# First stage: latents turned by one VectorE transpose and 32 DMAs per block in place of four TensorE transposes

## The chip, the cores and the metric

The kernel runs on one core of a Trainium2 chip. The metric is the device time of one execution in microseconds, the median of several runs; lower is better. The engines are named as in the profile: PE (TensorE matmul) with PEld (its weight loads), DVE (VectorE), ACT (ScalarE), POOL (GpSimd) and SP (SyncE, here only a queue that issues DMAs).

## The reference

The model is two layers over x of 16 x 256 x 256 in float32: a cross-attention of a resampler, a mixture of experts with two of eight experts per token, a second cross-attention, and a gated linear attention. Only the first cross-attention matters here. For each of the 16 batch entries it computes

```python
l = layer_norm(layernorm(x), ln2_g, ln2_b)          # latents, 256 x 256
c = layer_norm(ctx_1024, ln1_g, ln1_b)              # context, 77 x 256
q = l @ Wq                                          # 16 heads of 64
k, v = split(concatenate([c, l], axis=1) @ Wkv)     # 333 keys and values
out = softmax(q k^T / 8) v @ Wo
x = x + tanh(g_xattn[0]) * out
```

Every product contracts over the 256 features, so the normed latents are needed with the features on the partitions: 256 tokens x 256 features have to be turned. After the turning each feature is one partition, and the gain and bias of the second norm are one multiplication and one addition per partition.

## The kernel before

All of it is float32. The first stage (`stage0_fast`) goes through 64 units (b, g): batch entry b from 0 to 15 and, inside it, group g of four heads from 0 to 3. A unit has scores and their exponentials (`scores`), sums of the exponentials on POOL (`sums`), the values of the unit before it (`values`: PE products `o`, then a reciprocal `rd` and a product `oT` on DVE), and the queries and keys of the next unit (`heads`: PE products `qk`, copied by ACT and DVE). The other work is hung between these by hand. Unit (b, 1) also turns the latents of b + 1 (`turn`) and projects the output of b - 1 (`project`); unit (b, 2) computes the values' operands of b + 1 (`all_values`: PE products `v` from the turned latents `kvT`). The routing of the second layer for b - 1, b - 2 and b - 3 is spread over the units by three tables, which `run` reads: `ahead_of` (ahead of the scores), `behind_scores` and `behind_values`, lines 763 to 769. In unit (b, 2), for instance, `ahead_of` puts `route.weigh` and `route.stats`, short DVE work, which ends with the `mv` of the statistics, ahead of the scores.

What is recorded on an engine through `dve`, `act`, `pool` and `pe` keeps the program's order on that engine (`Pinned`, line 42; nearly all of it shows up under line 50). SP's DMAs (`nc.sync`) are not tied; a scheduler places them, and each waits for the DMA eight before it.

`turn(b)`, line 612, is what the change touches. `normed_all` (line 604) has left the latents of b in `xn`, two tiles of 128 tokens x 256 features, on ACT. PE turns them by four 128 x 128 transposes into a PSUM pair named `tr`, and DVE scales the two halves from there into `kvT[b][:, k, :256]` with gain and bias (line 627). The context's rows come 128 at a time, so only ten of the 16 entries bring new ones (0, 1, 3, 4, 6, 8, 9, 11, 13, 14). For these, PE transposes `cn` too, twice, into the same pair, DVE scales them into `ctxT`, and the values of the context (`v` from `ctxT`) come ahead of the values of the latents. ACT copies an entry's context columns from `ctxT` to the end of its `kvT` (line 633). `y`, line 601, is the result of the first of the two norms; its buffer has one slot, written by `normed_y(b + 2)` in unit (b, 3) and last read by `normed_all(b + 1)` in unit (b, 0).

In the last stage the same kind of turning stands already (`turn_ahead`, line 1685): one DVE transpose of all 32 x 32 squares of 128 x 512, then 16 DMAs of 32 partitions x 4 x 32 elements that carry the squares to their places.

Of the kernel before, what the change touches and what calls it, by code (L numbers as in the profile page):

```python
# [10 lines left out]
F32 = mybir.dt.float32  # L11
I32 = mybir.dt.int32
AF = mybir.ActivationFunctionType
ALU = mybir.AluOpType
# [3 lines left out]
P = 128  # L18
B, S, D = 16, 256, 256
# [4 lines left out]
V_LN1G, V_LN1B, V_LN2G, V_LN2B, V_QB, V_KB, V_NW, V_ONE, V_GATE, V_N = 0, 2, 4, 6, 8, 10, 12, 13, 14, 18  # L24
# [49 lines left out]
def layers(ctx: ExitStack, tc: tile.TileContext, t, out, check):  # L74
    nc = tc.nc
# [6 lines left out]
    def const(name, shape, dtype=F32):  # L82
        return cp.tile(list(shape), dtype, tag=name, name=name)
# [30 lines left out]
    def c_count(j):  # L114
        return min(P, c_rows - P * j)

    def c_pieces(b):

        lo, hi = b * S2, (b + 1) * S2
        return [(j, max(lo, P * j) - P * j, max(lo, P * j) - lo, min(hi, P * j + P) - max(lo, P * j))  # L120
                for j in range(lo // P, (hi - 1) // P + 1)]
# [7 lines left out]
    vec = const("vec", [P, V_N])  # L129
# [34 lines left out]
    ident = const("ident", [P, P])  # L164
# [10 lines left out]
    dve, act, pool, pe = (Pinned(tc, x) for x in (nc.vector, nc.scalar, nc.gpsimd, nc.tensor))  # L175
# [43 lines left out]
    def normed(dst, src, mv, rs, p=P, n=2):  # L219
        for i in range(n):  # L220
            act.activation(dst[:, i, :], src[:, i, :], AF.Identity, bias=rs[:p, 1, i:i + 1],
                           scale=rs[:p, 0, i:i + 1])
# [36 lines left out]
    NK, KC = S + S2, 111  # L259
# [289 lines left out]
    if fast:  # L549
        route = Route()  # L550
# [15 lines left out]
    def stage0_fast():  # L566
        with ExitStack() as sx:
            w1 = sx.enter_context(tc.tile_pool(name="f0w1", bufs=1, reuse_waits="tile"))
            w2 = sx.enter_context(tc.tile_pool(name="f0w2", bufs=2, reuse_waits="tile"))
# [3 lines left out]
            def pair(name):  # L573
                return pairs.tile([P, 2, 512], F32, tag="ps", name=name)
# [6 lines left out]
            xn, cn, kvT, v, oT, ctxT = {}, {}, {}, {}, {}, {}  # L581
# [5 lines left out]
            y, mvs, tallies = {}, {}, []  # L587
# [16 lines left out]
            def normed_all(b):  # L604
                xn[b] = w1.tile([P, 2, D], F32, tag="xn", name="xn")
                normed(xn[b], y.pop(b), *mvs.pop((b, "y")))
                if b in c_new:
                    n = c_count(c_new[b])
                    cn[b] = w1.tile([P, 1, D], F32, tag="cn", name="cn")
                    normed(cn[b][:n], cs[b][:n].unsqueeze(1), *mvs.pop((b, "c")), n, 1)  # L610

            def turn(b):
                kvT[b] = w2.tile([P, 2, NK], F32, tag="kvT", name="kvT")
                both = pair("tr")
                j = c_new.get(b)
                n = 0 if j is None else c_count(j)
                for k in range(2):
                    ps = both[:, k, :]
                    for i in range(2):
                        pe.transpose(ps[:, i * P:(i + 1) * P], xn[b][:, i, k * P:(k + 1) * P], ident)  # L620
                    if n:
                        pe.transpose(ps[:, S:S + n], cn[b][:n, 0, k * P:(k + 1) * P], ident[:n, :n])
                if n:
                    ctxT[j] = w2.tile([P, 2, P], F32, tag="ctxT", name="ctxT")
                for k in range(2):
                    ps = both[:, k, :]
                    dve.tensor_scalar(kvT[b][:, k, :S], ps[:, :S], vec[:, V_LN2G + k:V_LN2G + k + 1],
                                            vec[:, V_LN2B + k:V_LN2B + k + 1], ALU.mult, ALU.add)
                    if n:
                        dve.tensor_scalar(ctxT[j][:, k, :n], ps[:, S:S + n], vec[:, V_LN1G + k:V_LN1G + k + 1],  # L630
                                                vec[:, V_LN1B + k:V_LN1B + k + 1], ALU.mult, ALU.add)
                for j, at, to, n in c_pieces(b):
                    act.copy(kvT[b][:, :, S + to:S + to + n], ctxT[j][:, :, at:at + n])
# [120 lines left out]
            def project(b):  # L754
                both = pair("proj")
                for i in range(2):
                    for m in range(8):
# [3 lines left out]


            ahead_of = {0: [(norm_y, 1), (route.exps, -2)], 1: [(route.choose, -2)],
                        2: [(route.weigh, -2), (route.stats, -1)], 3: [(route.place, -2), (norm_x, 2), (norm_c, 2)]}
            behind_scores = {0: [(normed_all, 1), (route.scatter, -3, 1)],
                             1: [(route.scatter, -3, 2)],
                             2: [(route.norm, -1), (route.scatter, -3, 3)],
                             3: [(normed_y, 2), (route.scatter, -2, 0)]}
            behind_values = {2: [(route.ranks, -2, bank)], 3: [(route.logits, -1, bank)]}

            def run(steps, b, g):
                for f, d, *a in steps.get(g, ()):
# [14 lines left out]
            warm(y[0][:, 1, :], 3)  # L787
            normed_all(0)
            turn(0)
            all_values(0)  # L790
            heads(0, 0, 0)
# [3 lines left out]
            for n, (b, g) in enumerate(units):  # L795
# [20 lines left out]
                if g == 1 and b + 1 < B:  # L816
                    turn(b + 1)
# [34 lines left out]
    if fast:  # L852
        stage0_fast()
        s_banks = ctx.enter_context(ExitStack())
        pss = s_banks.enter_context(tc.tile_pool(name="f012ps", bufs=4, space=PSUM, reuse_waits="tile"))

        def shared_bank(name):
            return pss.tile([P, 512], F32, tag="ps", name=name)

    else:  # L860
        stage0()
# [1389 lines left out]
```

## Time and profile before

| | |
|---|---|
| three runs | median 1838.59 us, 1833.2 to 1842.05 |
| the profiled execution | 1836.71 us, its span 1834.8 us |
| granted PE clock in it | 0.995 |
| first stage, from the weights in place | 85 to 960 us |
| turning in the first stage | 64 transposes of latents and 20 of context rows on PE, 32 scalings of 128 x 256 on DVE |

The page lists the busy time of each engine, the course of it over the span, and the groups of instructions by kind. Start times count from the beginning of the span. A group's line gives its number of instructions, its busy time, the mean duration of one, and the idle time of the engine ahead of it with the one that ended it. A busy PE is not a PE at its peak: matmuls overlap, so the price of one is the distance from its start to the next.

### The profile page before, as it was taken

To read this page: it belongs to the slowest core of one execution; us is meant where nothing else is said; L and a number is where in the kernel's file an instruction comes from. 1 tells how busy PE (TensorE), PEld (TensorE's weight loads), DVE (VectorE), ACT (ScalarE), POOL (GpSimd) and SP (SyncE) were. 2 spreads that over 40 slices of the span, in tenths; PEclk is the share of its full clock that TensorE was granted. 3 is DMA by queue.
4 is the path that set the end of the run, shared out by engine and by line. 5 is a ranking of instruction groups with operands and counts; after the bars stand their busy time and mean duration, and the time that the engine had idled before them with its cause. 6 is when DMAs were issued, how large, how long until landed. Compare 5 with 4: busy or idle time off the path is not lost.

```text
span 1834.8 us, 35411 instructions
## 1 busy us (share of the span) xinstructions
PE 1802.7 (98%) x13930; PEld 1246.4 (68%) x13930; DVE 1138.6 (62%) x2695; ACT 832.4 (45%) x1727; POOL 1014.3 (55%) x1001
## 2 busy tenths in 40 slices
PE   8999999999999999999999999999999999999997
PEld 5666666666666666666777866656777777777775
DVE  3345656666656666666475388866666666666664
ACT  4433345343453334434343488744543454445432
POOL 3654766567666576656743766314454445444533
PEclk9999999999999999999999999999999999999999
DMA  9800010000010000000067933100111111111110
GB/s 298 235 1 22 16 35 13 28 17 20 27 35 10 29 20 10 28 24 17 13 221 246 251 56 48 21 3 11 38 28 36 29 37 28 34 31 32 33 31 26
DMA packets 110361, 98.05 MB, mean 53 GB/s; under 512 B 43835, under 2 KB 97763, under 8 KB 109673
## 3 DMA queue, kind: packets, MB, share of 16 engines
q1 hardware_dynamic: 97897, 78.91, 14.5%
q0 software_dynamic: 12288, 16.79, 4.5%
q8 instruction: 112, 1.84, 0.4%
q14 instruction: 64, 0.52, 0.1%
HBM read 52.03 MB, written 38.41 MB: 49 GB/s over the span
## 4 chain that ended last, share of the span: by engine, by line
PE 84%; POOL 7%; DVE 3%; issue 2%; ACT 2%; SPq 1%; DMA 1%; POOLq 0%; ACTq 0%; DVEq 0%
PE o L50 11%; PE qk L50 11%; PE v L50 9%; PE sc L50 8%; PE proj L50 7%; PE kq L1637 6%; PE sc L1637 6%; PE gq L1637 4%; POOL es L50 4%; PE ex L50 3%; PE v L1637 3%; PE o L1637 3%; PE proj L1637 2%; PE low L1637 2%; PE gz L1637 2%
## 5 line engine op out<-in xcount | busy, mean ns | idle before, releaser
L50 POOL TENSOR_SCALAR rs<-mv 128x2 f32<-128x2 f32 (+2 forms) x85 | 16.2, 190 | 404.4 <-DVE mv L50 402.6
L50 DVE RECIPROCAL rd<-o 128x256 f32<-128x256 f32 x64 | 112.3, 1754 | 155.0 <-PE o L50 155.0
L50 ACT ACTIVATE e<-sc 128x1024 f32<-128x1024 f32 (+1 forms) x192 | 181.5, 1015 | 18.5 <-PE sc L50 18.5
L50 POOL TENSOR_TENSOR at<-at,at 128x768 f32<-128x768 f32 x63 | 114.1, 1812 | 134.3 <-DVE at L50 134.3
L50 PE MATMUL sc<-qk 64*128 64x256 f32 (+1 forms) x1536 | 183.1, 384 | 0.5 <-DVE qk L50 0.5
L50 PE MATMUL o<-e,v 128*32 128x256 f32 (+1 forms) x3072 | 177.9, 379 | 0.0
L50 PEld LDWEIGHTS sc<-qk 64*128 64x128 f32 (+1 forms) x1536 | 132.0, 172 | 55.1 <-issue 26.8
L50 POOL TENSOR_TENSOR esum<-esum,es 128x512 f32<-128x512 f32 x128 | 163.2, 1275 | 10.0
L50 PE MATMUL qk<-kvT,wkv 128*128 128x333 f32 x512 | 164.3, 443 | 0.0
L50 POOL TENSOR_TENSOR es<-e 128x1024 f32<-128x1024 f32 x64 | 151.3, 2364 | 12.0 <-ACT e L50 9.0
L50 ACT ACTIVATE qk<-qk 128x256 f32<-128x256 f32 x128 | 48.7, 381 | 232.2 <-PE qk L50 232.2
L50 POOL TENSOR_TENSOR es<-es,e 77x1024 f32<-77x1024 f32 x64 | 150.3, 2349 | 5.0
L50 PEld LDWEIGHTS o<-e,v 128*32 128x32 f32 (+1 forms) x3072 | 99.8, 110 | 66.4
L50 DVE TENSOR_TENSOR at<-sc,amask 128x768 f32<-128x768 f32 x64 | 61.2, 957 | 133.7 <-PE sc L1637 78.2
L50 PE MATMUL qk<-kvT,wq 128*128 128x256 f32 x512 | 134.6, 385 | 0.0
L50 DVE COPY qk<-qk 128x333 f32<-128x333 f32 x128 | 64.6, 505 | 94.8 <-ACT qk L50 93.4
L50 POOL DMA_INDIRECT x<-rows_out,pos x64 | 100.9, 1577 | 35.6 <-issue 16.5
L50 PEld LDWEIGHTS qk<-kvT,wq 128*128 128x128 f32 x512 | 94.3, 189 | 35.1 <-issue 9.6
L50 PEld LDWEIGHTS qk<-kvT,wkv 128*128 128x128 f32 x512 | 97.2, 190 | 30.0
L50 PE MATMUL proj<-wo0h,oT 128*128 128x256 f32 x512 | 113.7, 380 | 0.3 <-DVE oT L50 0.3
L50 PE MATMUL v<-wkv,kvT 128*128 128x512 f32 x256 | 113.1, 595 | 0.0
L50 PEld LDWEIGHTS proj<-wo0h,oT 128*128 128x128 f32 x512 | 96.0, 190 | 13.9 <-issue 0.8
(267 smaller groups left out, 3920.8 us busy)
## 6 DMA issues: line engine op xcount, KB each, us to landing
rows<-zero SPq DMA_DIRECT2D x16, 640.0 KB
xin<-rows SPq DMA_DIRECT2D x16, 640.0 KB
r<-rms SPq DMA_DIRECT2D x30, 256.0 KB
rows_out<-y SPq DMA_DIRECT2D x16, 384.0 KB
v<-vctx SPq DMA_DIRECT2D x15, 308.0 KB
x<-in_x_dram SPq DMA_DIRECT2D x16, 256.0 KB
rows_out<-y SPq DMA_DIRECT2D x16, 256.0 KB
out_dram<-x SPq DMA_DIRECT2D x15, 256.0 KB
```

The lines of the kernel that those rows point to most:

```text
L50: x = getattr(self.engine, name)(*a, **k)
L1637: tc.keep_in_program_order(nc.tensor.matmul(*a, **k))
```

## The change

For entries b of 2 and more the latents are no longer turned on PE. `squares_moved(b + 1)` runs behind the values in unit (b, 0): one DVE transpose turns each of the 64 squares of 32 x 32 of the 128 x 512 tile, each at its own position, into `z` (named `turned`, in the buffer of `y`), and 32 DMAs on SP's queue carry the squares to their places in `kvT`, each DMA taking the two squares that lie at the same place in the two halves of the features, 32 partitions x 2 x 32 elements. `scaled(b + 1)` runs in unit (b, 2), behind `route.weigh` and `route.stats` and ahead of that unit's scores in the program's order: two DVE operations multiply and add in place in `kvT`. `turn` keeps the transposes of context rows, and for b below 2 all of it as it was.

```diff
+            def squares_moved(b):
+
+                if b < 2:
+                    return
+                z = w1.tile([P, 2 * D], F32, tag="y", name="turned")
+                dve.transpose(z, xn[b].rearrange("p i d -> p (i d)"))
+                kvT[b] = w2.tile([P, 2, NK], F32, tag="kvT", name="kvT")
+                to, at = kvT[b][:, :, :S].rearrange("p k (i s) -> p i k s", i=2), z.rearrange("p (i k d) -> p i k d", i=2, k=2)
+                for q in range(0, P, 32):
+                    for r in range(0, P, 32):
+                        for i in range(2):
+                            nc.sync.dma_start(out=to[r:r + 32, i, :, q:q + 32], in_=at[q:q + 32, i, :, r:r + 32])
+
+            def scaled(b):
+
+                if b < 2:
+                    return
+                for k in range(2):
+                    dve.tensor_scalar(kvT[b][:, k, :S], kvT[b][:, k, :S], vec[:, V_LN2G + k:V_LN2G + k + 1],
+                                      vec[:, V_LN2B + k:V_LN2B + k + 1], ALU.mult, ALU.add)
+
             def turn(b):
-                kvT[b] = w2.tile([P, 2, NK], F32, tag="kvT", name="kvT")
-                both = pair("tr")
                 j = c_new.get(b)
                 n = 0 if j is None else c_count(j)
+                if b < 2:
+                    kvT[b] = w2.tile([P, 2, NK], F32, tag="kvT", name="kvT")
+                if b < 2 or n:
+                    both = pair("tr")
                 for k in range(2):
-                    ps = both[:, k, :]
-                    for i in range(2):
-                        pe.transpose(ps[:, i * P:(i + 1) * P], xn[b][:, i, k * P:(k + 1) * P], ident)
+                    for i in range(2 if b < 2 else 0):
+                        pe.transpose(both[:, k, i * P:(i + 1) * P], xn[b][:, i, k * P:(k + 1) * P], ident)
                     if n:
-                        pe.transpose(ps[:, S:S + n], cn[b][:n, 0, k * P:(k + 1) * P], ident[:n, :n])
+                        pe.transpose(both[:, k, S:S + n], cn[b][:n, 0, k * P:(k + 1) * P], ident[:n, :n])
...
-                for k in range(2):
+                for k in range(2 if b < 2 or n else 0):
                     ps = both[:, k, :]
-                    dve.tensor_scalar(kvT[b][:, k, :S], ps[:, :S], vec[:, V_LN2G + k:V_LN2G + k + 1],
-                                            vec[:, V_LN2B + k:V_LN2B + k + 1], ALU.mult, ALU.add)
+                    if b < 2:
+                        dve.tensor_scalar(kvT[b][:, k, :S], ps[:, :S], vec[:, V_LN2G + k:V_LN2G + k + 1],
+                                          vec[:, V_LN2B + k:V_LN2B + k + 1], ALU.mult, ALU.add)
...
-                        2: [(route.weigh, -2), (route.stats, -1)], 3: [(route.place, -2), (norm_x, 2), (norm_c, 2)]}
+                        2: [(route.weigh, -2), (route.stats, -1), (scaled, 1)], 3: [(route.place, -2), (norm_x, 2), (norm_c, 2)]}
...
-            behind_values = {2: [(route.ranks, -2, bank)], 3: [(route.logits, -1, bank)]}
+            behind_values = {0: [(squares_moved, 1)], 2: [(route.ranks, -2, bank)], 3: [(route.logits, -1, bank)]}
```

## The prediction

> **What bounds the kernel now.** I read the page's busy shares first, then the busy time by stretch, TensorE's waits in the first stage, the chain that ended last, and at the end one block of the first stage on the time axis.
>
> ```profile
> PE 1802.7 (98%) x13930; PEld 1246.4 (68%) x13930; DVE 1138.6 (62%) x2695; ACT 832.4 (45%) x1727; POOL 1014.3 (55%) x1001
> ...
> PE 84%; POOL 7%; DVE 3%; issue 2%; ACT 2%; SPq 1%; DMA 1%; POOLq 0%; ACTq 0%; DVEq 0%
> ```
> ```profile
> 85.00:960.00 875.00, 871.64 (x7121) 586.82 (x7120) 536.89 (x1324) 356.11 (x693) 560.31 (x501) 1.00 0.10 30
> ```
> ```profile
> PE o L50 <- POOL es L50: 1.8, 8, 0.4
> PE rank L50 <- DVE hs L50: 0.4, 1, 0.4
> ```
>
> The second fence's columns are the stretch in us, its length, the busy time of PE, PEld, DVE, ACT and POOL, the clock and the DMA share. From 85 to 960 us, the first stage once the weights are in, PE is busy 871.6 of 875 us at full clock. Its longest wait in total there is 1.8 us for POOL's sums (last fence: total, times, longest). The DMA engines stand at 10%. So this stage is paced by PE's own work. An instruction taken from PE is worth its PE time, as long as nothing new makes PE wait.
>
> **What goes.** Block 7 (latents of b = 7, turned in unit (6,1)) brings no new context rows. This is its part of PE's timeline, with the group of these transposes by tile above it:
>
> ```profile
> L50 PE MATMUL tr<-ident,xn x128: 271/273/332, 9.2 to 1190.0; 128*128 128x128 f32 x128
> ```
> ```profile
> 376.13 2.78 PE L50 MATMUL o<-e,v 128*32 128x256 f32 x48
> 378.85 0.66 PE L50 MATMUL tr<-ident,xn 128*128 128x128 f32 x4
> 379.34 7.07 PE L50 MATMUL proj<-wo0h,oT 128*128 128x256 f32 x32
> ```
>
> The 273 ns of one transpose overlap the next; its price is the step from start to start. Four cost 379.34 - 378.85 = 0.49 us. In blocks with context rows six span 0.71 us, 0.11 us a step, and two remain, so 0.44 us goes. Of the 14 blocks (2 to 15), 8 are of the second kind: 8 x 0.44 + 6 x 0.49 = 6.5 us. VectorE loses two PSUM-to-SBUF scalings of 0.53 us per block; they lie beside the 7 us projection, so that is worth nothing. Nor is the freed PSUM pair: PE shows no wait for a bank.
>
> **What is added and moved, in block 7.** The path is new: VectorE transpose, 32 DMAs on SP's queue, VectorE scaling, then PE's value matmuls. These are the places it has to fit into:
>
> ```profile
> 370.65 0.69 DVE L50 TENSOR_TENSOR oT<-o,rd 128x512 f32<-128x512 f32 x1
> 371.43 0.51 DVE L50 COPY qk<-qk 128x333 f32<-128x333 f32 x1
> ...
> 393.53 0.30 DVE L50 BATCH_NORM_AGGREGATE mv<-bst 128x2 f32<-128x6 f32 x2
> 396.41 1.76 DVE L50 RECIPROCAL rd<-o 128x256 f32<-128x256 f32 x1 [2.58 <-PE o L50]
> ```
> ```profile
> 395.66 1.08 POOL L50 DMA_INDIRECT rows<-xw,pos  x1 [0.18 <-issue]
> 396.77 2.36 POOL L50 TENSOR_TENSOR es<-e 128x1024 f32<-128x1024 f32 x1
> ```
>
> The transpose stands behind oT (ends 371.34); the scaling stands behind the last mv (ends 393.83) and ahead of rd. VectorE is idle there for 2.58 us.
>
> The last stage already turns its input this way, with 16 DMAs per block, so durations are to be had:
>
> ```profile
> L50 DVE STREAM_TRANSPOSE turned<-xn x14: 699/711/712, 1258.4 to 1740.6; 128x512 f32<-128x512 f32 x14
> ```
> ```profile
> 1335.18 10.32 SPq L1693 DMA_DIRECT2D xnT<-turned  x16
> ```
> ```profile
> 1346.97 0.89 PE L1637 MATMUL low<-xnT,la 128*128 128x256 f32 x3 [0.23 <-DMA xnT<-turned]
> ```
>
> *Transpose:* 0.71 us, to 372.05. It holds back the first key copy, 371.43 to about 372.05; that then ends at 372.56, ahead of the scores at 372.89 that read it. Cost 0, cover 0.3 us. Its input from ScalarE is ready 0.3 to 3.5 us ahead of it in every block.
>
> *DMAs:* 16 issues take 10.32 us, 0.645 each. The last of the 16 starts at about 1344.9 and PE goes on at 1346.97, so landing takes 2.1 us. The new DMAs move half the pieces each (32 x 2 x 32 against 32 x 4 x 32). The nearest rows are flat in size, as SP's `low` copy of 64 pieces took 0.60 us, so I take 0.645; low end 0.58 (SP's `lowd` copy, 0.54, and 0.04 between two). A few issues of the last stage were 0.1 to 0.7 us late, which I book as 0.3 us per block. First issue at 372.1, last start 31 x 0.645 = 20.0 later at 392.1, landed at 394.2 to 394.5. Nothing urgent stands behind them on SP's queue: in block 6 the next entries, context writes, come at 343.0, and SP would be done at 334. The context load ahead of them goes out within 0.2 us of oT's end (312.54 against 312.43 in block 6).
>
> *Scaling:* PE's 0.49 us lets VectorE reach it at 393.3, so it waits about 1 us for the DMAs. Queued behind it are rd and oT, wanted at 396.41 - 0.49 = 395.9, and PE's value matmuls, wanted at the same time. Two scalings SBUF to SBUF: between the one such row of this width (gbo, 0.35 us) and what they took from PSUM (0.53); I take 0.4 as in the same form with two scalars (xn, 0.41). They end at 395.0 to 395.3, 0.6 to 0.9 us early. In blocks with context rows the values of the context come first (3.5 us), and the cover is wider.
>
> *Waits:* in program order the first value matmul now carries waits for four DMA semaphores more. A wait on PE's queue takes 0.05 us in this trace, so 0.2 us per block if all is exposed and none if PE's queue runs ahead. I take 0.1 in the six blocks that have no context values before it: 0.6 us.
>
> Sum: 6.5 - 0.6 = 5.9 us less, with ends of 3.6 and 6.5. The profiled execution took 1836.7 us (span 1834.8), which gives 1830.8; it lies 1.9 us under the median of the three runs, so the median goes from 1838.6 to 1832.7.
>
> **Where a rule speaks against it.** The Trainium skill, "DMA: Bandwidth & Descriptors", section "Rules for kernel authors", has small transfers coalesced, since under 64 KB one pays mostly overhead; these are 8 KB. If each paid the 2.1 us that the trace shows to landing one after the other, 32 would take 67 us, 43 us past the 24 us from 372 to 396, and 14 blocks would lose some 600 us. The row (16 in 10.32 us) shows the overhead overlapped, with only the issue in series. I take the row.
>
> For a late scaling there is no row. VectorE's transposes took 0.71 us beside POOL and the same without, while its operations with two SBUF inputs were held until POOL's ended:
>
> ```profile
> L50 DVE TENSOR_TENSOR h<-rq,rc x32: 174/1120/3107, 142.5 to 954.7; 128x16 f32<-128x16 f32 x32
> ```
>
> "SBUF — State Buffer", section "Who interferes with whom", says that a `tensor_scalar` between SBUF tensors may take the port pair shared with POOL, and that whichever of the two comes second is blocked for the whole instruction. By the transposes' row a late scaling costs its lateness alone; by the rule and h's row up to 3.1 us more. No trace here shows it for this form; I take the rule for the rival below.
>
> **Rivals.**
> 1. *Likeliest, 0.55:* all of it hides, 1832.7.
> 2. *Part of the gain comes back, 0.22:* the DMAs land 0.5 to 1.5 us later in some blocks. Six blocks without context values at about 1 us each take 6 us back: 1838.6. For it: a cover of only 0.6 to 0.9 us. Against it: the even pace of 0.645.
> 3. *Late landing meets POOL, 0.15, slower:* POOL's scatter starts at 395.66 - 0.49 = 395.2 and its es add ends at 399.13 - 0.49 = 398.6. If the DMAs land after 395.2, an issue pace of over 0.67 us, the first scaling is held to 398.6 and the second ends at 399.4 or later. PE stands from 395.9, 3.5 us in each of six blocks = 21 us; the eight others want the latents 3.5 us later and just escape. Less the 5.9: 1854. Held a second time, to the end of the next add (2.35 us), it is 1868.
> 4. *The change doesn't do what it says, 0.08:* PE's saved time reappears as a wait for POOL, whose sums already hold PE up to 0.4 us in the unit ahead of the transposes: 1838.6. Against it: after them POOL has 9 us of slack, and its next chain starts from VectorE work that PE paces.
>
> **How the numbers follow.** About 0.5% (9 us) is what a measurement of this kernel can tell from no change. The likeliest case lies 5.9 us under the median, inside that bound, and the three runs spread over 9 us. So 0.17 of the 0.55 may read as faster, and nothing else does; rival 3 and a tail of rival 2 make slower 0.16; the rest, 0.67, is within it. The range runs from 1826 (largest gain and a low draw) to 1847; above it lies most of rival 3.
>
> **What would show it.** PE's list should have 56 fewer transposes and no wait of values for kvT over 0.3 us. SP should show 32 issues in about 20.6 us per block. The scaling should take 0.35 to 0.45 us, after an idle time of about 1 us put down to the DMAs, and rd should keep its wait for PE. Wrong would be an issue pace over 0.67, scalings of over 1 us, or rd starting without a wait for PE.

## The result and the profile after

The changed kernel took 1851.91 us, median of 5 runs (1848.18 to 1852.93), beside 1838.34 us for the kernel before (5 runs, 1833.2 to 1842.05): ratio 1.0073, 95% interval 1.0055 to 1.0091. By the medians that is 13.6 us slower, where 1832.7 was predicted. The profiled execution took 1851.91 us, its span 1850.0 us.

The page's busy times and the chain of the changed kernel:

```profile
PE 1803.1 (97%) x13874; PEld 1239.9 (67%) x13874; DVE 1166.5 (63%) x2709; ACT 834.0 (45%) x1727; POOL 1015.5 (55%) x1001
...
PE 74%; SPq 8%; POOL 6%; DVE 5%; issue 2%; DMA 2%; ACT 1%; DVEq 0%; POOLq 0%; ACTq 0%
```

PE's list has the 56 transposes fewer, 13874 against 13930, but its busy time is the same: some products take longer, where the clock falls (below). SP's queue has come into the chain: 8% against 1%, so the chain now runs through the issuing of DMAs. The same two views of the first stage as before, stretch and PE's waits (total, times, longest):

```profile
85.00:970.00 885.00, 869.77 (x7030) 578.70 (x7029) 559.58 (x1311) 354.07 (x685) 559.40 (x499) 0.99 0.12 32
```
```profile
PE v L50 <- issue: 6.7, 3, 2.9
PE v L50 <- DVE kvT L50: 4.8, 5, 1.8
PE o L50 <- POOL es L50: 2.0, 8, 0.4
```

PE stands 15 us of this stretch where it stood 3. Two lines are new, 11.5 us in eight waits, all ahead of the values `v`, which read the scaled latents. A wait put down to "issue" has no releaser in the trace; these stand at the same place as the others, ahead of the same products.

By stages: the first product `ex` of the second layer starts at 934.30 us before and at 949.99 after, 15.7 later. From there to the last stage's first product `low` it is 266.4 and 266.5 us, from there to the end 634.1 and 633.5. So all of the lost time lies in the first stage, and there in five of 14 blocks. (The equal times of the last stage hide a difference. Leaving out the last 7 us of both, the kernel before ran there for 10.2 us at half clock and the changed one not at all; its waits of `low` for turned input are longer, 6.1 us in total against 3.7. The second question below comes back to this.) The period of a block (first projection to first projection), and in the changed kernel the time of the first scaling and both durations, in us from the start of the block's transpose:

| block | before | after | difference | first scaling at | both took |
|---|---|---|---|---|---|
| 2 | 55.10 | 58.82 | +3.7 | 24.17 | 1.19, 2.50 |
| 5 | 55.48 | 55.17 | -0.3 | 23.43 | 0.41, 0.41 |
| 6 | 58.44 | 59.05 | +0.6 | 24.89 | 3.22, 2.49 |
| 7 | 55.48 | 62.00 | +6.5 | 25.04 | 2.61, 2.49 |
| 10 | 55.47 | 55.16 | -0.3 | 23.63 | 0.41, 0.41 |
| 12 | 55.48 | 57.28 | +1.8 | 23.96 | 0.41, 3.36 |
| 15 | 54.51 | 60.95 | +6.4 | 25.16 | 2.48, 2.49 |

Blocks 3, 4, 8, 9, 11, 13 and 14, all with context rows, gained 0.42 to 0.50 each. In blocks without context rows PE wants the scaled latents 24.7 after the transpose, in the others 28.7. Block 3's scalings were slow too (2.49, 2.50), at no cost, since PE wants them so much later there. Gains of 3.9 and losses of 19.1 make 15.2 of the 15.7.

Block 7 is the clearest. VectorE, POOL and PE there, on the time axis:

```profile
396.38 0.30 DVE L50 BATCH_NORM_AGGREGATE mv<-bst 128x2 f32<-128x6 f32 x2
...
398.52 1.08 POOL L50 DMA_INDIRECT rows<-xw,pos  x1 [0.17 <-issue]
...
399.53 5.02 DVE L50 TENSOR_SCALAR kvT<-kvT,vec 128x256 f32<-128x256 f32 x2 [2.86 <-DMA kvT<-turned]
399.63 2.35 POOL L50 TENSOR_TENSOR es<-e 128x1024 f32<-128x1024 f32 x1
402.06 2.34 POOL L50 TENSOR_TENSOR es<-es,e 77x1024 f32<-77x1024 f32 x1
```
```profile
399.00 0.29 PE L50 MATMUL rank<-before,hs 128*32 128x64 f32 x8
402.24 1.85 PE L50 MATMUL v<-wkv,kvT 128*128 128x512 f32 x2 [2.94 <-issue]
404.61 2.07 PE L50 MATMUL v<-wkv,kvT 128*128 128x512 f32 x2 [0.51 <-DVE kvT L50]
```

The last `mv` ends at 396.68. VectorE then waits 2.86 us for the DMAs, and the two scalings, 0.41 us each where nothing disturbs them, take 5.02 together, 2.61 and 2.49 in the table. The first starts just ahead of POOL's first `es` addition and ends 0.16 us behind it, at 402.14; the second ends 0.15 us behind the second addition, at 404.55. PE, done at 399.29, waits 2.94 us and 0.51 more for the second half. An undisturbed block, 10, for comparison:

```profile
576.59 0.73 DVE L50 TENSOR_SCALAR kvT<-kvT,vec 128x256 f32<-128x256 f32 x2 [1.46 <-DMA kvT<-turned]
577.70 1.76 DVE L50 RECIPROCAL rd<-o 128x256 f32<-128x256 f32 x1 [0.38 <-PE o L50]
```

2.94 and 0.51 do not make 6.5. The rest is in PE's clock, last but two of the columns (PEclk), in block 7 before, during and after the wait:

```profile
388.00:399.20 11.20, 11.20 (x110) 7.83 (x108) 4.71 (x20) 4.83 (x9) 3.00 (x6) 1.00 0.09 13
402.20:409.10 6.90, 6.35 (x8) 2.23 (x9) 6.78 (x11) 0.00 (x0) 4.73 (x3) 0.52 0.00 0
409.10:420.00 10.90, 10.90 (x54) 6.80 (x56) 6.88 (x25) 6.30 (x14) 0.00 (x0) 0.99 0.00 0
```

After the wait PE runs at half clock for 6.8 us, which is 3.4 us of work lost. 2.94 + 0.51 + 3.4 less the 0.3 that undisturbed blocks of this kind gain is the 6.5 of the table. Block 15 repeats it; block 2 has 3.4 us at half clock.

### The profile page after: what moved, and what is told of

It reads as the page before. It is cut to its first block, busy times and chain, and to the rows that moved or that the text cites. A ratio compares the mean times of both kernels' runs of the same rounds, so it can differ in the third digit from the quotient of the medians.

```text
span 1850.0 us, 35901 instructions
## 1 busy us (share of the span) xinstructions
PE 1803.1 (97%) x13874; PEld 1239.9 (67%) x13874; DVE 1166.5 (63%) x2709; ACT 834.0 (45%) x1727; POOL 1015.5 (55%) x1001
## 3 DMA queue, kind: packets, MB, share of 16 engines
q8 instruction: 111, 1.82, 0.4%
## 4 chain that ended last, share of the span: by engine, by line
PE 74%; SPq 8%; POOL 6%; DVE 5%; issue 2%; DMA 2%; ACT 1%; DVEq 0%; POOLq 0%; ACTq 0%
PE o L50 10%; PE qk L50 9%; PE v L50 9%; PE sc L50 7%; PE proj L50 5%; PE kq L1660 5%; SPq L623 5%; PE sc L1660 5%; PE gq L1660 3%; PE ex L50 3%; POOL es L50 3%; SPq L1716 3%; PE v L1660 3%; PE o L1660 2%; PE proj L1660 2%
## 5 line engine op out<-in xcount | busy, mean ns | idle before, releaser
L50 ACT ACTIVATE e<-sc 128x1024 f32<-128x1024 f32 (+1 forms) x192 | 181.6, 1016 | 18.1 <-PE sc L50 18.1
L50 PE MATMUL v<-wkv,kvT 128*128 128x512 f32 x256 | 121.9, 628 | 11.5 <-issue 6.7
```

The source lines that it names most:

```text
L50: x = getattr(self.engine, name)(*a, **k)
```

## The experiments

Three theories stood after this profile. **1:** the DMAs land late, and POOL's additions then hold the scaling ("two-port" in the texts below: the plain form, which by the rule weighed in the prediction may take the port pair shared with POOL). **2:** late landing alone stops PE. **3:** what is added costs everywhere, by its mere presence. Where not said otherwise a kernel is an edit of the changed one. "Stage end" is the start of the first `ex`: 934.30 before, 949.99 after.

**Without the turning (no_turn).**

```diff
-                z = w1.tile([P, 2 * D], F32, tag="y", name="turned")
-                dve.transpose(z, xn[b].rearrange("p i d -> p (i d)"))
...
-                            nc.sync.dma_start(out=to[r:r + 32, i, :, q:q + 32], in_=at[q:q + 32, i, :, r:r + 32])
+                if b >= 2:
+                    kvT[b] = kvT[b - 2]
...
```

The entry `(scaled, 1)` goes from the table as well.

> This leaves the turning of the latents out for entries of 2 and more (they take those of two entries before), and with it the transpose, the DMAs and the scaling; the context is turned as before. All theories: what PE's transposes were worth, 6 us under the kernel before, about 1832. If it is 1836 or more, the transposes were never worth their time and the change could not have gained.

Measured: 5569.45 us. The total says nothing: with stale latents it goes through further layers after the first pass (832 products `ex` against 320). Its first pass can be read: stage end 929.39, 4.9 us ahead of before. That is all that PE's transposes were worth in this stage, against 6.5 in my sum (5.9 after the waits that I allowed for).

**Without gain and bias (no_scale).**

```diff
-                        2: [(route.weigh, -2), (route.stats, -1), (scaled, 1)], 3: [(route.place, -2), (norm_x, 2), (norm_c, 2)]}
+                        2: [(route.weigh, -2), (route.stats, -1)], 3: [(route.place, -2), (norm_x, 2), (norm_c, 2)]}
```

> This leaves the gain and bias of the second norm out for entries of 2 and more; transpose and 32 DMAs stay, and the values wait for the DMAs directly. Theory 1 (the scaling comes late and is then held by POOL's additions): no scaling, no hold, so 1832 to 1836. Theory 2 (the DMAs' landing is late enough by itself to stop PE): 1846 to 1852, as with the scaling. Theory 3 (the added transposes and DMAs slow other work everywhere): 1846 to 1852, spread over all blocks.

Measured: 1836.32 us (20 runs) beside 1836.31, ratio 0.9999 [0.9990, 1.0007]; stage end 929.39. The transposes and all 448 DMAs are still there, and the stage is as short as without them: PE never waits for the values' operands in it. Theory 3 falls, and so does theory 2 in the strong form that gave 1846 to 1852 here. The total is that of before all the same, though the stage ends 4.9 us earlier: a second question, taken up below.

**Scaling on ScalarE (act_scales), and on VectorE in the form that also sums (acc).**

```diff
-                    dve.tensor_scalar(kvT[b][:, k, :S], kvT[b][:, k, :S], vec[:, V_LN2G + k:V_LN2G + k + 1],
-                                      vec[:, V_LN2B + k:V_LN2B + k + 1], ALU.mult, ALU.add)
+                    act.activation(kvT[b][:, k, :S], kvT[b][:, k, :S], AF.Identity, bias=vec[:, V_LN2B + k:V_LN2B + k + 1],
+                                   scale=vec[:, V_LN2G + k:V_LN2G + k + 1])
```
```diff
-                                      vec[:, V_LN2B + k:V_LN2B + k + 1], ALU.mult, ALU.add)
+                                      vec[:, V_LN2B + k:V_LN2B + k + 1], ALU.mult, ALU.add,
+                                      accum_out=st.tile([P, 1], F32, tag="acc", name="acc"))
```

In `act_scales` the call is also moved from the units' `ahead_of` table, where it stood behind `route.stats`, to the head of the third unit's entries in `behind_scores`.

> The scaling is done by ACT, behind the exponentials of the same unit; everything else as changed. Theory 1: ACT is not held by POOL, the scaling ends about 1.1 us behind the landing, PE loses at most 1 us in the five late blocks: 1833 to 1838. Theory 2 and 3: 1848 or more, since the landing is as late as before.

> The scaling stays on VectorE at its place, but as the form that also writes out the sum of each row; the sums are not used. Theory 1, if the hold comes from the two-port form alone: one scaling takes about 0.5 us and none takes over 1 us, time 1833 to 1838. If the hold is not a matter of the form, five blocks keep scalings of 2.5 us and the time is 1850 to 1853. Theory 2 and 3: 1850 or more.

Measured: act_scales 1836.59 us, ratio 1.0010 [1.0000, 1.0020], stage end 932.06; acc 1837.79 us, ratio 1.0015 [1.0005, 1.0024], stage end 931.86. In acc only the form of the instruction differs, with a read of the accumulator of 0.08 us behind each. Its block 7 is a twin of the one above:

```profile
393.57 1.08 POOL L50 DMA_INDIRECT rows<-xw,pos  x1 [0.18 <-issue]
...
394.59 0.54 DVE L50 TENSOR_SCALAR_CACHE_REDUCE kvT<-kvT,vec 128x256 f32<-128x256 f32 x1 [2.85 <-DMA kvT<-turned]
394.67 2.37 POOL L50 TENSOR_TENSOR es<-e 128x1024 f32<-128x1024 f32 x1
...
395.05 0.54 DVE L50 TENSOR_SCALAR_CACHE_REDUCE kvT<-kvT,vec 128x256 f32<-128x256 f32 x1
...
395.24 3.24 PE L50 MATMUL v<-wkv,kvT 128*128 128x512 f32 x7 [0.88 <-ACT rxn L50]
```

The DMAs land just as late (2.85 us of waiting against 2.86), and POOL stands at the same distance (scatter 1.02 ahead of the scaling, against 1.01). But the scaling takes 0.54 us beside `es`, and PE waits 0.88 us where it waited 2.94. Over all 28 the form took 534 to 541 ns. Its stage ends 2.5 us after that of no_scale: that is the price of the late landing with a scaling behind it that nothing holds. The other 18.1 us, to 949.99, are the hold and what follows it. The rule of the skill that I had weighed ("SBUF — State Buffer", "Who interferes with whom") leaves out precisely the form that writes out its accumulator; this pair of runs bears it out.

**Fewer DMAs (diagonals), and both cures together (diag_act).** Squares that keep their place need no DMA: behind the values of unit (b, 1), four VectorE transposes of 32 x 128 turn these 16 squares straight into `kvT`, and 24 DMAs remain. diag_act also has the scaling on ScalarE, as in act_scales.

```diff
-                        for i in range(2):
+                        for i in range(2 if q != r else 0):
...
+                for q in range(0, P, 32):
+                    dve.transpose(to[q:q + 32, :, :, q:q + 32], at[q:q + 32, :, :, q:q + 32])
...
-            behind_values = {0: [(squares_moved, 1)], 2: [(route.ranks, -2, bank)], 3: [(route.logits, -1, bank)]}
+            behind_values = {0: [(squares_moved, 1)], 1: [(diagonals, 1)], 2: [(route.ranks, -2, bank)], 3: [(route.logits, -1, bank)]}
```

> The 8 of 32 DMAs whose squares stay on their own partitions are replaced by four VectorE transposes straight into place, behind the values of the unit between; 24 DMAs are left. Theory 1 (32 issues, some of them stretched, end too late): the last landing moves from 23 to 25 us behind the transpose to 17 to 19, ahead of VectorE's 22; no wait for DMAs in the scaling, no scaling over 1 us, stage 5 us shorter than before: 1831 to 1833 against 1836.3. Theory 3 (by-cost of the transposes and DMAs): 1840 or more.

> As the run with the four direct transposes, with the scaling on ACT behind the exponentials. Theory 1: once the DMAs are early it is the same which engine scales: within 2 us of that run, 1831 to 1834. If the scaling on VectorE still costs anything there, this one is faster by it.

Measured: diagonals 1834.98 us (13 runs) beside 1835.87, ratio 0.9995 [0.9985, 1.0005], stage end 929.21; diag_act 1834.87 us, ratio 0.9998 [0.9991, 1.0005], stage end 929.40. The groups in diagonals, by tile (min, median and max in ns, then first and last start):

```profile
L623 SPq DMA_DIRECT2D kvT<-turned x336: 585/595/1623, 85.0 to 841.9; - x168
L50 DVE STREAM_TRANSPOSE kvT<-xn x56: 291/304/310, 100.3 to 842.2; 32x128 f32<-32x128 f32 x56
L50 DVE TENSOR_SCALAR kvT<-kvT,vec x28: 406/411/414, 105.1 to 848.1; 128x256 f32<-128x256 f32 x28
```

Issues as long as 1.6 us are still there, but the train is about five us shorter (15.5 us from first to last start on average, 20.8 in the changed kernel), and all 28 scalings took 0.41 us in the plain form. Being early is as good as being immune. The stage gained 5.1 us, the total 0.9 by the medians: no change clear of noise, and not the 3 to 5 us that I expected.

**Four more DMAs at the end of each block (late4).** They carry squares that are carried already.

```diff
+                for r in (0, 32):
+                    for i in range(2):
+                        nc.sync.dma_start(out=to[r:r + 32, i, :, :32], in_=at[:32, i, :, r:r + 32])
```

> The first four DMAs of a block are issued once more at its end, so that the landing comes 4 x 0.65 = 2.6 us later in every block; nothing else differs from the change. Theory 1: now nearly all 14 blocks have both scalings held by POOL's two additions, 2.5 us each; the six blocks without context values lose 6 to 7 us each (stall and the half clock after it), the eight others about 2: 1836 - 5 + 40 + 16 = about 1887, at least 1870. Theory 2 (lateness alone): 2.6 us more in the six blocks, none in the others: 1852 + 16 = 1868 or less.

Measured: 1880.51 us (4 runs), ratio 1.0241 [1.0225, 1.0257], stage end 976.57. The group of the scalings and PE's waits for them, from 85 to 930 us:

```profile
L50 DVE TENSOR_SCALAR kvT<-kvT,vec x28: 502/2226/2520, 110.9 to 893.6; 128x256 f32<-128x256 f32 x28
```
```profile
PE v L50 <- DVE kvT L50: 28.6, 19, 3.2
```

With the four DMAs more, every block is hit: not one of the 28 took 0.41 us, 2226 ns is the median, and PE ran at half clock in six stretches between 112 and 894 us, where the kernel before has none in this stage. Theory 1 has its second side: the hold goes with earlier DMAs and grows with later ones.

**The second question: where the 4.9 us went (both, last_only).** In the profiled executions the last stage waits more for its own turned input, which comes by 16 DMAs on the same queue. Before:

```profile
PE low L1637 <- DMA xnT<-turned: 3.7, 4, 2.6
```

No_scale, whose first stage is 4.9 us shorter, and the changed kernel, whose first stage is 15.7 us longer:

```profile
PE low L1660 <- DMA xnT<-turned: 7.4, 9, 2.3
```
```profile
PE low L1660 <- DMA xnT<-turned: 6.1, 8, 2.3
```

So the last stage's turning was given direct squares too, 12 DMAs in place of 16: on top of diagonals (both), and on the kernel before by itself (last_only).

```diff
-                        nc.sync.dma_start(out=to[r:r + 32, :, q:q + 32], in_=y[q:q + 32, :, r:r + 32])
+                        if q != r:
+                            nc.sync.dma_start(out=to[r:r + 32, :, q:q + 32], in_=y[q:q + 32, :, r:r + 32])
+
+            def turned_diagonals(b):
+
+                to, at = xnT[b].rearrange("p k (i s) -> p (k i) s", i=2), xn[b].rearrange("p k (i d) -> p (k i) d", i=2)
+                for q in range(0, P, 32):
+                    dve3.transpose(to[q:q + 32, :, q:q + 32], at[q:q + 32, :, q:q + 32])
...
-                    2: [(gate_logs, 1, 1), (turn_ahead, 2), (normed_out, -1, 0), (normed_out, -1, 1)]}
+                    2: [(gate_logs, 1, 1), (turn_ahead, 2), (turned_diagonals, 2), (normed_out, -1, 0), (normed_out, -1, 1)]}
```

> The direct transposes in the last stage too, whose 16 DMAs become 12, beside the first stage with 24. Theory 1, carried over: PE's waits for the turned input in the last stage (3.7 us in 4 waits before, 7.4 in 9 in another run) go, and the half clock behind the longest: 2 to 6 us under the run with the first stage alone, 1826 to 1831. If VectorE's added 1.2 us per block is on the last stage's path, 10 us or more above it instead.

> The kernel before with the last stage's turning alone changed: the four squares of 32 x 32 that keep their place are turned by VectorE straight to the place where they are read, so 12 DMAs carry the rest there instead of 16; the first stage is that of before. It tells how much of the gain of the run with both stages changed belongs to the first stage. If the first stage's 4 to 6 us were real and were only taken back by the last stage's waits for its turned input, this gives those waits' 4 us alone: about 1832 to 1833, some 5 us over the run with both. If the first stage is worth nothing in the total, it equals the run with both: 1826 to 1828. At most 1836 (nothing) if the last stage's waits are worth nothing by themselves. The trace should show no wait of the low products for the turned input, and a first stage that ends where it ends before (the second layer's first ex at about 934).

Measured: both 1825.77 us (5 runs), ratio 0.9951 [0.9938, 0.9965]; last_only 1829.47 us (6 runs), ratio 0.9969 [0.9957, 0.9981]. Neither trace has a wait of `low` for its input. The two intervals overlap, and the runs shared no chip; so both kernels were run once more side by side.

> The kernel with both stages changed, again, side by side with the kernel in which only the last stage is changed, on the same chip: the difference of the two is the first stage's turning alone, with no wait of the last stage for its turned input in either. By the trace of the first stage it should be 4 to 5 us less than its neighbour; if the first stage is worth nothing in the total, the two are equal within 1.5 us.

> The kernel with only the last stage changed, again, side by side with the kernel in which both are: 4 to 5 us above it if the first stage's gain is real in the total, within 1.5 us of it if not.

Measured, beside 1835.48 us for the kernel before: both_pair 1823.24 us (6 runs, 1821.49 to 1827.91), ratio 0.9929 [0.9914, 0.9944]; last_pair 1827.26 us (6 runs, 1826.47 to 1829.85), ratio 0.9958 [0.9942, 0.9973]. The difference is 4.0 us; resampling the two sets of six gives 1.1 to 7.2. So the first stage's turning off PE is worth about what its stage end says (929.64 against 934.22 in these two traces, 4.6 us) once the last stage does not stand on its DMAs. The two profiled executions come out the other way, 1827.91 and 1826.68 us, mainly because that of both_pair has 10.2 us at half clock between 1206 and 1234 us and that of last_pair none there. As an estimate without it, span times granted clock of each run has medians of 1817.5 and 1821.1 us, 3.6 us apart.

That the waits grow is not because the first stage is shorter, since the changed kernel and late4, whose first stages are longer, have them as well (late4: 6.6 us in 6). What the traces show is where the fetches of instructions fall (last section). Each of these traces has 26 fetches between the first and the last of the last stage's DMAs. With the first stage as before, 11 of the 224 issues there overlap one and 3 take over 0.8 us. In the seven kernels with the first stage changed and the last as it was (no_turn left out) it is 20 to 23 issues, and 7 to 10. In before a fetch comes about every 257 PE instructions (median, weight loads counted), and the first stage's change takes away 112 of them, 56 transposes and their weight loads, so that the fetches move against the last stage's DMAs. That this is the cause is inferred: no run moved the fetches alone. The version with both stages changed beats both kernels of this study.

## Why the prediction was wrong, point by point

- **What goes from PE** was right in kind and too large in sum, 4.9 us (no_turn) against 6.5. Blocks with context rows gained 0.42 to 0.50 us (0.44 predicted). Blocks without gained 0.31 where undisturbed (0.49 less 0.1 for waits predicted), and no more in no_turn, where no DMA is waited for: the price of the four transposes was too high, not the waits too low.
- **The transpose at no cost** held: in block 7 it took 0.70 us, and the key copy behind it ended at 375.59, ahead of the scores at 376.13.
- **The failed step: the landing**, "A few issues of the last stage were 0.1 to 0.7 us late, which I book as 0.3 us per block", with 2.1 us to land, and so "landed at 394.2 to 394.5". Two terms of it were too small. From first to last start the 32 issues took 20.2 to 22.2 us, mean 20.8, where 20.0 + 0.3 was booked. And the scaling started 1.9 to 2.7 us after the last issue in 12 blocks, but 3.7 in blocks 7 and 15. Block 7's scaling so came about 2 us later than the sum had it (25.04 after the transpose against 22.9 to 23.2), with a cover of 0.6 to 0.9. Its 32 issues, as the trace has them, took 21.21 us in place of 20.6; the landing, 3.7 us against 2.1, did the rest:

```profile
375.22 21.21 SPq L623 DMA_DIRECT2D kvT<-turned  x32
```

- **Rule or row for the DMAs:** the row was right. A train of 32 takes 20.8 us and not the 67 of small transfers that pay their landing one by one.
- **The scaling** was right where free (0.41 us against 0.4). But the sum booked 0.4 us whenever it came, and a late one took up to 3.4. Lateness by itself would still have left a gain in the stage (acc ends it 2.4 us ahead of before); the rule that I kept for the rival only was the one that decided.
- **Rival 3 is what happened**, and with 1854 us it was 2 us off. Its place and mechanism are those of the trace. Its point was not: "an issue pace of over 0.67 us" came in some blocks only (block 7 had 0.665), because a late landing needs no slow pace. And its sum was right by luck, through two errors: I had six blocks at 3.5 us; two of them (5 and 10) escaped, and the two worst lost 6.4 and 6.5, since the half clock after the wait was not in my sum. The last stage's even pace, which the prediction holds against rival 2, made late issues look rare. Three in 224 were over 0.8 us there in the trace of before; in the changed kernel's two stages it is 26 in 672, and with 32 in a row each of the 14 blocks has at least one gap of 1.0 to 1.95 us between two issues.
- **Rival 4** came true in a form I had not named: in kernels without the hold, the saved time was taken back in the last stage, by longer waits for DMAs there, and not at POOL's sums.

## What to carry to other kernels

When a chain of DMAs is to hide in a gap of PE, compare its cover with the latest landing seen in the trace and not with the mean: here 0.6 to 0.9 us of cover met a spread of 2.0 us in the issues and 1.8 in the landing. If the first instruction behind such a chain is a VectorE operation of the form that was held here, lateness is multiplied: here it cost the rest of POOL's addition and again the next one, and a PE wait of 2.9 us cost another 3.4 in clock. Shorten the chain, or use a form or an engine that was not held. A stage's gain is proved at the stage's end first; whether it reaches the total is a second measurement, and here it took the removal of the waits in the last stage.

## What the runs showed of the hardware

**Late issues go with instruction fetches.** The trace records 111 fetches of instructions for the changed kernel, of 16 KB and about 1.1 us each, as packets on a queue of their own (another queue has smaller ones). In before, after, no_scale, act_scales and acc together, 112 of the squares' DMA issues took over 0.8 us; every one overlaps such a fetch. Of the 2,680 that overlap none, the longest took 0.735 us. And landings: in after and acc the scaling started 3.5 to 3.8 us after the last issue in just those five of 28 blocks in which a fetch began 1.1 to 1.3 us behind that issue, and by 2.7 us at the latest in the others. The Trainium skill, "Runtime: NRT & Kernel Launch", section "Instruction fetch mechanics", has the fetch mostly hidden; for a queue that issues DMAs back to back these traces say otherwise. That the fetch is the cause is inferred: no run changed the fetches.

**The clock falls after less than 3 us of waiting.** The Trainium skill, "TensorE: Matmul & The Clock Gate", section "Part 1: The HAM clock gate (the "warmup" mystery)", puts the fall at an idle window of about 3.4 us. Here a wait of 2.94 us was followed by 6.8 us at half clock, and in before one of 2.61 us by 3.4 us: the clock of before from 1271.4 us on, right behind that wait,

```profile
1271.40:1274.80 3.40, 3.34 (x8) 2.75 (x9) 0.00 (x0) 0.00 (x0) 0.00 (x0) 0.50 0.02 5
```

is 0.50. The length of the two stretches, 3.4 and 6.8, fits the page's window; the idle time needed does not. Shorter waits did it too: in acc, act_scales, no_scale, diagonals and diag_act the first wait of `low`, 2.3 us, has 3.4 us at half clock behind it. Yet in the changed kernel the same wait, 2.27 us up to 1283.9, has none. The place in time explains it: within each trace all changes of the clock lie whole steps of 3.41 us apart. Where PE stood for 2.06 us or more within one such step, half clock followed every time; where it stood for 1.25 to 1.82 us, it did not, and the wait up to 1283.9 is cut by the edge of a step into 1.5 and 0.8 us. This leaves out the stretch between 1049 and 1236 us, where the clock fell in some traces with less waiting; that is not explained, and differs from run to run of one kernel (last_only 10.2 us at half clock, last_pair, the same program, none).
